# Attention projections of two tiles at a time as seven block products, with streamed weight pieces

## The chip, the cores and the metric

The kernel runs on one core of a Trainium2 chip. The metric is the device time of one execution in microseconds; several executions were timed, and one more was recorded by the hardware profiler. All data are fp32. TensorE is called PE in the profile, VectorE DVE, ScalarE ACT, GpSimd POOL and SyncE SP; SP issues most of the transfers.

## The reference

The reference runs four small networks on 64 sequences of 32 rows of 512 numbers (16 tiles of 128 rows). The kernel has them in three layers and a tail:

- layer 0: a weight chosen per sequence, a feed-forward block with two routed experts, a layer norm;
- layer 1: a gated feed-forward block with low-rank updates per sequence, and a routed low-rank block;
- layer 2: attention. Each sequence has 512 cached keys (16 pages of 32) and 32 new ones;
- the tail: a routed low-rank block, a matrix per sequence, and a last product.

The change concerns layer 2. Cut to what matters, it computes for every sequence:

```python
q, k, v = x @ Wq.T, x @ Wk.T, x @ Wv.T        # 32, 8 and 8 heads of 128 numbers
q, k = rope(rmsnorm(q) * q_norm), rope(rmsnorm(k) * k_norm)
keys, values = pages_of(cache) + [k, v]        # 544 in all, masked beyond the length
out = softmax(q @ keys.T / sqrt(128)) @ values @ Wo.T
```

Each key head serves four query heads.

## The kernel before

Layer 2 takes the heads in two halves (`HALVES`), each with 4 key heads and 16 query heads. A step is one half of the heads for one tile of 128 rows, so there are 32 steps, and two consecutive steps are a **pair** of tiles. A step has 16 **turns**, one per sequence (4) and key head (4). In each turn PE transposes the probabilities (L684, `prT_ps`), starts the scores of the turn after the next (L900, `sc`, one buffer in PSUM), and multiplies values with probabilities (L689, `po`). DVE adds the mask and finds the row's extreme (L905), ACT takes the exponential (L907), DVE the reciprocal (L909) and the scaling (L912), and ACT copies the transposed probabilities (L918). Behind every second sequence come products with the new keys' values; before them DVE copies the new values to their places (L722).

Each turn has two **slots**, in which other work is put between the instructions of the turn. Lists of slot numbers written out by hand say what goes where. That work is:

- the **projections** of the next step, by `Projection.product`. A step has six of 128x512 outputs: `v`, `k` and four groups of `q`. Each sums four products of 128x512 in a PSUM tile with tag `mm` (two buffers), two products in each of two slots. All weights of a half lie in SBUF (six tiles of 1 MB) and are loaded at the start of the half by `weights`;
- the rotation of `q` and `k` by `rotated`. ACT squares out of PSUM (L728), DVE sums the squares (L730, L731), POOL takes the inverse root (L128). DVE multiplies by the rotary tables `cos` (L741) and `sin` (L744, two halves) out of PSUM, and POOL adds and scales (L747, L748). `turned` then transposes the result on PE (`qkT_ps`), and ACT copies it (L801, L803);
- the **output product** of the pair before (`Outputs`). It already uses a scheme of seven block products in place of eight: two tiles of rows are cut into blocks of a 2x2 matrix, so is the weight, and sums of blocks are multiplied. Its weights come as pieces of 0.5 MB (`wo`), four ahead; the pieces that are sums of blocks were made in layer 1 by `sum_up` and stored in DRAM (`wo_sums`).

Keys come as 16 transfers of 64 KB per sequence on SP's queue (`load_keys`, L100), weight pieces on the same queue in a fixed order (`load_by`). Values come by four indirect transfers per sequence, which POOL issues (L715). `later` holds loads that follow in the next slots, two per slot.

PE's instructions run in the order in which they are written (`on_pe`); for the other engines the framework chooses the order from the dependencies and its own estimates.

In layer 1 `sum_up` has three parts (`rows` loads four blocks, `add` makes four sums of 128x256 on POOL (L289 to L292), `store` writes them back). Two such sums are made in each of the eight groups.

Of the kernel before, what the change touches and what calls it, by code (L numbers as in the profile page):

```python
# [33 lines left out]
P = 128  # L34
# [18 lines left out]
SCALE = 1.0 / float(np.sqrt(HD))  # L53

# [217 lines left out]
def sum_up(c, pool, sums, h, k):  # L272


    nc, a = c.nc, c.a
    H = D // 2
    w, t = [], []

    def rows():
        w.append(pool.tile([P, 4, H], F32, name="sum", bufs=3))  # L280
        for n in range(2):
            at = (h * HQP + n * HQP // 2 + k) * HD
            nc.sync.dma_start(w[0][:, 2 * n:2 * n + 2, :].rearrange("p a b -> p (a b)"),
                              a["WoT"][at:at + HD, :])

    def add():
        t.append(pool.tile([P, 4, H], F32, name="sum", bufs=3))
        (b11, b12, b21, b22), (t1, t2, t3, t4) = ([v[0][:, n, :] for n in range(4)] for v in (w, t))
        nc.gpsimd.tensor_tensor(t1, b12, b11, ALU.subtract)  # L289
        nc.gpsimd.tensor_tensor(t3, b22, b12, ALU.subtract)  # L290
        nc.gpsimd.tensor_tensor(t2, b22, t1, ALU.subtract)
        nc.gpsimd.tensor_tensor(t4, b21, t2, ALU.subtract)  # L292

    def store():
        nc.sync.dma_start(sums[h][:, k], t[0])

    return rows, add, store


def layer1(c, kp, x_in, x_out, sums):  # L300
# [12 lines left out]
    with ExitStack() as ctx:  # L313
# [193 lines left out]

        groups[0].x(0)
# [3 lines left out]
        for g, new in enumerate(groups):  # L512
            old = groups[g - 1] if g else None
            then = groups[g + 1] if g + 1 < len(groups) else None
            sum0, sum1 = (sum_up(c, sum_p, sums, *divmod(2 * g + i, HQP // 2)) for i in range(2))
            new.features(0)
            sum0[0]()
            if old:
                old.choose(0)
            new.features(1)  # L520
            if old:
                old.choose(1)
            new.features(2)
# [3 lines left out]
            sum0[1]()  # L527
            new.features(3)
# [4 lines left out]
            new.features(4)  # L533
# [6 lines left out]
            new.features(5)  # L540
            sum0[2]()
            sum1[0]()
            new.features(6)
            new.features(7)
            if then:
                then.x(0)
            new.features(8)
            if then:
                then.x(1)
            new.features(9)  # L550
            if then:
                then.firsts("x")
            sum1[1]()
            new.features(10)
            sum1[2]()
# [82 lines left out]
def attention(c, known, x_in, y_part, y_out, sums, tail):  # L638
# [13 lines left out]

    tc, nc, a = c.tc, c.nc, c.a
    half = HD // 2
    n_c = L // P
    with ExitStack() as outer:
        wvk = outer.enter_context(tc.tile_pool(name="l2_key_value_weights", bufs=1))
# [3 lines left out]
        wp = outer.enter_context(tc.tile_pool(name="l2_query_weights", bufs=1))  # L661
        op = outer.enter_context(tc.tile_pool(name="l2_output_weights", bufs=1))
# [6 lines left out]
        ws = {"v": wvk.tile([P, KC, HKP * HD], F32, name="wv"),  # L669
              "k": wvk.tile([P, KC, HKP * HD], F32, name="wk"),  # L670
              "q": [wp.tile([P, KC, D], F32, name=f"wq{g}") for g in range(HKP)]}
# [63 lines left out]
        def rotated(psrc, tab):  # L735

            src = psrc.rearrange("p (h d) -> p h d", d=HD)
            ct, st = tab
            rs = squares_and_root(src)
            r = qp.tile([P, REP, HD], F32, name="rot")  # L740
            nc.vector.tensor_tensor(r, src, ct.unsqueeze(1).to_broadcast([P, REP, HD]), ALU.mult)  # L741
# [5 lines left out]
            nc.gpsimd.tensor_tensor(r, r, tmp, ALU.add)  # L747
            last = nc.gpsimd.tensor_tensor(r, r, rs.unsqueeze(2).to_broadcast([P, REP, HD]), ALU.mult)  # L748
            return r, last.ins

        class Projection:


            def __init__(self, h, T, w):
                self.h, self.T, self.w = h, T, w
                self.r, self.acc = {}, {}
                self.first = "v"

            def load(self):
                self.xt = c.load(xp, "xt", [P, D], x_in(self.T))  # L760

            def tables(self):
                self.tabs = {}
                for n in ("q", "k"):
                    ct = qp.tile([P, 2, half], F32, name=n + "_cos")
                    st = qp.tile([P, 2, half], F32, name=n + "_sin")
                    for t, w_n, f in ((ct, norm[n][0], cos), (st, norm[n][1], sin)):
                        self.last_pool = nc.gpsimd.tensor_tensor(
                            t, w_n, f[:, self.T, :].unsqueeze(1).to_broadcast([P, 2, half]),
                            ALU.mult).ins  # L770
                    self.tabs[n] = tuple(t.rearrange("p u f -> p (u f)") for t in (ct, st))

            def x(self):
                pt = transposes("tq", "xT_ps", [self.xt[:, k * P:(k + 1) * P] for k in range(KC)])
                self.xT = xp.tile([P, KC, P], F32, name="xT")
                nc.scalar.copy(self.xT, pt)

            def product(self, what, u):

                n, g = (what, 0) if what in ("k", "v") else ("q", what)  # L780
                if what == self.first and u == 0:
                    self.qT = qp.tile([P, HKP, SEQ, REP, S], F32, name="qT")
                    self.kT = qp.tile([P, HKP, P], F32, name="kT_own")
                    self.v = qp.tile([P, HKP * HD], F32, name="v")
                if u == 0:
                    self.acc[what] = ps.tile([P, D], F32, tag="mm", bufs=2, name=f"p{n}")
                w = self.w[n][g] if n == "q" else self.w[n]
                part(self.acc[what], [(self.xT[:, k, :], w[:, k, :]) for k in (2 * u, 2 * u + 1)],
                     u == 0, u == 1)
                if u == 0:  # L790
                    return
                if what == "v":
                    nc.scalar.copy(self.v, self.acc[what])
                else:
                    self.r[what], self.last_pool = rotated(self.acc[what], self.tabs[n])

            def turned(self, what):
                r = self.r.pop(what)
                pt = transposes("tq", "qkT_ps", [r[:, m, :] for m in range(REP)])
                if what == "k":  # L800
                    nc.scalar.copy(self.kT, pt)  # L801
                else:
                    nc.scalar.copy(self.qT[:, what].rearrange("p j h s -> p h j s"),  # L803
                                   pt.rearrange("p h (j s) -> p h j s", j=SEQ))
# [11 lines left out]
        def wo_piece(h, m, u):  # L816
# [6 lines left out]
            else:  # L823
                src = sums[h][:, u * QH:(u + 1) * QH, {5: 0, 6: 1, 7: 2, 4: 3}[m], :]
# [63 lines left out]
        def scores(i, p, h, b, g):  # L888
# [7 lines left out]
            q = p.qT[:, g, b % SEQ].rearrange("p h s -> p (h s)")  # L896
# [56 lines left out]
        def weights(h, what):  # L953

            n, g = (what, 0) if what in ("k", "v") else ("q", what)
            heads = HQP if n == "q" else HKP
            at = h * heads * HD + g * D
            c.load_by(ws[n][g] if n == "q" else ws[n],
                      a[f"W{n}T"][:, at:at + D].rearrange("(k p) n -> p k n", p=P))

# [10 lines left out]
        projections = {s: Projection(h, T, ws) for s, (h, T) in enumerate(steps)}  # L971
# [47 lines left out]
        def projected(what, *then):  # L1019
            p.product(what, 0)  # L1020
            p.product(what, 1)
            for w in then:
                p.turned(w)
# [456 lines left out]
```

## Time and profile before

| what | value |
|---|---|
| median of 3 runs | 3651.27 us (3644.59 to 3653.99) |
| the profiled execution, own time | 3648.7 us |
| its span | 3646.9 us |
| granted TensorE clock | 0.998 |
| moved by DMA | 527 MB, 145 GB/s in the mean |
| layer 2, from the first to the last turn | 1087 to 3451 us |
| period of a pair of tiles | 149.4 us |

The span runs from the first to the last instruction. In a row of a group, the number behind `x` counts the instructions, then come their busy time, the mean of one in ns, and the time for which the engine stood idle before them, with what ended it. An fp32 product of PE is shown as two instructions. Consecutive instructions of an engine overlap a little, so the distance between two is less than the mean of one.

### The profile page before, as it was taken

The page shows a single profiled execution, that of the slowest core. Times are in us where ns is not written, and L with a number is a line of the kernel's source. Part 1 is how long each engine was busy: PE and PEld are TensorE (multiplying, and loading weights), DVE is VectorE, ACT ScalarE, POOL GpSimd, SP SyncE. Part 2 cuts the span into 40 slices and gives each one's busy share as a digit, 9 for nine tenths or more (in the row PEclk, how much of TensorE's full clock was granted, in tenths as well). Part 3 has the DMA queues.
Part 4 walks back from the last instruction along what each step waited for, and adds up shares of the span by engine and source line. Part 5 has one row for each costly group of instructions (what it writes and reads, how often), then busy time and mean ns, then how long its engine had stood idle before and what let it go on. Part 6 is the DMA issues. An engine that isn't in the chain of part 4 may idle for free.

```text
span 3646.9 us, 60352 instructions
## 1 busy us (share of the span) xinstructions
PE 3589.7 (98%) x19520; PEld 2665.6 (73%) x19520; DVE 1894.8 (52%) x4932; ACT 1296.2 (36%) x3046; POOL 1415.8 (39%) x1407
## 2 busy tenths in 40 slices
PE   8999999999999999999999999999999999999999
PEld 3444788888866777777777877778777788777855
DVE  5453222222236655666666656566666666666533
ACT  1111111111115544444444444444444444444311
POOL 0112430000025544555445454454555544545232
PEclk9999999999999999999999999999999999999999
DMA  5004541111124566555555565555555555556631
GB/s 211 24 27 170 171 152 55 50 45 36 38 93 133 149 186 185 155 171 153 185 183 153 181 219 179 179 151 182 174 181 169 156 186 178 170 175 201 218 97 62
DMA packets 527914, 527.15 MB, mean 145 GB/s; under 512 B 54162, under 2 KB 441234, under 8 KB 527602
## 3 DMA queue, kind: packets, MB, share of 16 engines
q1 hardware_dynamic: 480882, 371.21, 32.9%
q0 software_dynamic: 44416, 147.88, 12.6%
q10 hardware_dynamic: 2304, 4.20, 0.3%
q8 instruction: 159, 2.61, 0.3%
q14 instruction: 153, 1.25, 0.1%
HBM read 493.72 MB, written 29.36 MB: 143 GB/s over the span
## 4 chain that ended last, share of the span: by engine, by line
PE 85%; DVE 8%; ACT 2%; DMA 2%; issue 1%; SPq 1%; DVEq 0%; POOL 0%; another core or an unknown queue 0%; ACTq 0%; POOLq 0%
PE po L689 12%; PE sc L900 11%; PE gate_up L342 10%; PE pq L689 9%; PE py L689 9%; PE prT_ps L684 5%; PE pz L342 5%; PE po L1249 3%; PE ph L124 3%; PE pk L689 3%; PE pv L689 3%; PE pd L249 2%; DVE own_vt L722 2%; PE po L342 2%; DVE pr L905 1%; PE qkT_ps L684 1%
## 5 line engine op out<-in xcount | busy, mean ns | idle before, releaser
L715 POOL DMA_INDIRECT vt<-in_v_rows,v_rows x512 | 499.9, 976 | 594.6 <-PE po L689 484.2
L907 ACT ACTIVATE pr<-pr,low 128x544 f32<-128x544 f32 x512 | 383.5, 749 | 703.5 <-DVE low L905 630.4
L689 PEld LDWEIGHTS po<-prT,vt 128*128 128x128 f32 x4096 | 531.3, 192 | 111.1 <-issue 80.7
L900 PE MATMUL sc<-kt,qT 128*128 128x288 f32 (+1 forms) x2048 | 556.3, 394 | 5.5 <-ACT qT L803 1.7
L689 PE MATMUL po<-prT,vt 128*128 128x128 f32 x4096 | 543.9, 276 | 9.5 <-ACT prT L918 6.3
L905 DVE CUSTOM_DVE_ANT_0 pr<-sc,mask 128x544 f32<-128x544 f32 x512 | 368.8, 720 | 321.8 <-PE sc L900 288.5
L900 PEld LDWEIGHTS sc<-kt,qT 128*128 128x128 f32 x2048 | 370.6, 190 | 156.0 <-issue 62.0
L689 PE MATMUL pq<-wq,xT 128*128 128x512 f32 x1024 | 480.6, 592 | 0.0
L918 ACT COPY prT<-prT_ps 128x512 f32<-128x512 f32 x512 | 295.3, 577 | 202.1 <-PE prT_ps L684 147.6
L912 DVE TENSOR_SCALAR pr<-pr,low 128x512 f32<-128x512 f32 x512 | 341.1, 666 | 15.1
L684 PE MATMUL prT_ps<-ident,pr 128*128 128x128 f32 x2048 | 311.2, 275 | 0.1
L689 PEld LDWEIGHTS pq<-wq,xT 128*128 128x128 f32 x1024 | 185.8, 190 | 132.4 <-issue 125.3
L909 DVE RECIPROCAL low<-low 128x1 f32<-128x1 f32 x512 | 83.5, 163 | 340.8 <-ACT pr L907 305.7
L684 PEld LDWEIGHTS prT_ps<-ident,pr 128*128 128x128 f32 x2048 | 238.1, 142 | 7.9 <-issue 0.3
L689 PE MATMUL py<-wo,oT 128*128 128x256 f32 x1024 | 241.4, 379 | 0.0
L128 POOL TENSOR_TENSOR rs<-rs,minus_half 128x4 f32<-128x4 f32 x160 | 169.2, 1058 | 162.9 <-DVE rs L731 158.1
L910 ACT ACTIVATE own_pr<-pr,low 128x32 f32<-128x32 f32 x512 | 164.0, 320 | 131.0 <-DVE low L909 120.3
L747 POOL TENSOR_TENSOR rot<-rot,swapped 128x512 f32<-128x512 f32 x160 | 205.0, 1281 | 5.1 <-DVE swapped L744 3.9
L689 PEld LDWEIGHTS py<-wo,oT 128*128 128x128 f32 x1024 | 187.6, 190 | 21.9
L722 DVE COPY own_vt<-v 32x128 f32<-32x128 f32 x512 | 173.1, 338 | 38.3 <-PE po L689 13.9
L689 PE MATMUL py<-wo,o_sum 128*128 128x256 f32 x768 | 181.3, 379 | 2.1 <-DMA wo<-wo_sums 1.3
L426 DVE TENSOR_TENSOR sg<-sg,gate_up 128x256 f32<-128x256 f32 (+1 forms) x88 | 37.0, 421 | 276.0 <-ACT sg L425 276.0
(226 smaller groups left out, 5192.9 us busy)
## 6 DMA issues: line engine op xcount, KB each, us to landing
kt<-in_kT SPq DMA_DIRECT2D x2048, 64.0 KB
wo<-wo_sums SPq DMA_DIRECT2D x128, 512.0 KB
wo<-in_WoT SPq DMA_DIRECT2D x96, 512.0 KB
xt<-x SPq DMA_DIRECT2D x48, 256.0 KB
A<-in_A SPq DMA_DIRECT2D x64, 152.0 KB
sets<-in_cond0T SPq DMA_DIRECT2D x32, 256.0 KB
sum<-in_WoT SPq DMA_DIRECT2D x32, 256.0 KB
wo_sums<-sum SPq DMA_DIRECT2D x16, 512.0 KB
```

What stands on the lines that cost most here:

```text
L128: self.nc.gpsimd.tensor_tensor(t, t, self.minus_half[:, :n], ALU.pow)
L342: c.on_pe(nc.tensor.matmul(out, lhsT, rhs, start=start, stop=stop))
L684: c.on_pe(nc.tensor.transpose(pt[:, m, :], piece, c.ident))
L689: c.on_pe(nc.tensor.matmul(out, lhsT, rhs, start=first and i == 0, stop=last and i == len(pairs) - 1))
L715: nc.gpsimd.indirect_dma_start(out=vts[b % 2][:, n, :], out_offset=None, in_=a["v_rows"], in_offset=bass.IndirectOffsetOnAxis(ap=rows[h][: ...
L722: nc.vector.tensor_copy(own_vts[b % 2][g * S:(g + 1) * S, g % 2, :], v[j * S:(j + 1) * S, g * HD:(g + 1) * HD])
L747: nc.gpsimd.tensor_tensor(r, r, tmp, ALU.add)
L900: c.on_pe(nc.tensor.matmul(sc[:, lo + n * PSIZE:lo + m * PSIZE].rearrange("p (n k) -> p n k", k=PSIZE), q, kt[:, n:m, g, :], start=True, s ...
L905: nc.vector.tensor_tensor_reduce(pr[:, :NK], sc[:, lo:lo + NK], masks[h, b], -SCALE, 3.0e38, ALU.add, ALU.min, low[:, 0:1])
L907: nc.scalar.activation(pr[:, :NK], pr[:, :NK], AF.Exp, bias=low[:, 0:1], scale=-1.0, accum_out=low[:, 1:2])
L912: nc.vector.tensor_scalar(pr[:, :L], pr[:, :L], low[:, 2:3], None, ALU.mult)
L918: nc.scalar.copy(prT, pt)
```

## The change

A pair of tiles is projected together. The 2x2 blocks are the two tiles (rows) by the two halves of the 512 input numbers; the weight's blocks are the two halves of the input by two column blocks of 512. The column blocks form three groups (`GB = 3`) per half of the heads: `k` with `v`, and `q` in two groups of two. Each group takes seven products of 256 by 512 (two 128x512 products each) instead of eight.

- `x_sums` makes the four sums of the tiles' blocks on POOL (128x256 each). `product` multiplies one of them with a weight piece. Its result is copied by ACT (products 1 and 5) or added to an earlier one by DVE out of PSUM (2, 6, 3, 7 and 4); after products 3 and 7 POOL adds two results in SBUF. Results lie in SBUF, and `rotated` now works there in place.
- Weights no longer stay in SBUF. They come as 21 pieces of 0.5 MB per pair, four ahead, by `wp_piece`: blocks of the weights, or sums of blocks made in layer 1.
- In layer 1, `all_sums` makes 40 sums instead of 16, five per group.
- All projections of pair n+1 stand in the first step and the second step of pair n, at slots 16 to 51 of 64 (8 to 52 in the first pair). The output products of pair n-1 stand at slots 0 to 15 and 53 to 61, in the last pair at 1 to 43. Before the first turn, all of the first pair is projected.
- The tail's weights take the places of other tiles, and are loaded earlier in the last pair.

```diff
-        def rotated(psrc, tab):
-            src = psrc.rearrange("p (h d) -> p h d", d=HD)
+        def rotated(t, tab):
+            src = t.rearrange("p (h d) -> p h d", d=HD)
             ct, st = tab
             rs = squares_and_root(src)
-            r = qp.tile([P, REP, HD], F32, name="rot")
-            nc.vector.tensor_tensor(r, src, ct.unsqueeze(1).to_broadcast([P, REP, HD]), ALU.mult)
             tmp = wk.tile([P, REP, HD], F32, name="swapped")
...
-            nc.gpsimd.tensor_tensor(r, r, tmp, ALU.add)
-            last = nc.gpsimd.tensor_tensor(r, r, rs.unsqueeze(2).to_broadcast([P, REP, HD]), ALU.mult)
+            nc.vector.tensor_tensor(src, src, ct.unsqueeze(1).to_broadcast([P, REP, HD]), ALU.mult)
+            nc.gpsimd.tensor_tensor(src, src, tmp, ALU.add)
+            nc.gpsimd.tensor_tensor(src, src, rs.unsqueeze(2).to_broadcast([P, REP, HD]), ALU.mult)
...
+        def wp_tile(name="wp", **kw):
+            return op.tile([P, K2, D], F32, name=name, tag="wp", bufs=4, **kw)
+
+        def wp_piece(h, g, m):
+            w = wp_tile()
+            if m in (1, 2, 3):
+                k, n = {1: (0, 0), 2: (1, 0), 3: (1, 1)}[m]
+                src = column_blocks(a, h, g)[n][k * K2 * P:(k + 1) * K2 * P, :] \
+                    .rearrange("(k p) n -> p k n", p=P)
+            else:
+                src = sums["in", h][:, g, {5: 0, 6: 1, 7: 2, 4: 3}[m]]
+            c.load_by(w, src)
+            return w
...
+            def x_sums(self):
...
+                nc.gpsimd.tensor_tensor(s1, x21, x22, ALU.add)
+                nc.gpsimd.tensor_tensor(s2, s1, x11, ALU.subtract)
+                nc.gpsimd.tensor_tensor(s3, x11, x21, ALU.subtract)
+                nc.gpsimd.tensor_tensor(s4, x12, s2, ALU.subtract)
...
+            def product(self, g, m):
+                (x11, x12), (_, x22) = self.blocks
+                lhs = {1: x11, 2: x12, 3: self.s[3], 4: x22, 5: self.s[0], 6: self.s[1], 7: self.s[2]}[m]
+                w = wps.pop(0)
+                acc = ps.tile([P, D], F32, tag="mm", bufs=2, name="pq" if g else "pkv")
+                part(acc, [(lhs[:, k, :], w[:, k, :]) for k in range(K2)], True, True)
+                d = self.d = {} if m == 1 else self.d
+                if m in (1, 5):
...
+                    nc.scalar.copy(d[at], acc)
                     return
...
+                nc.vector.tensor_tensor(d[to], acc, d[other], ALU.add)
+                if m == 3:
+                    nc.gpsimd.tensor_tensor(d[0, 1], d[0, 1], d[1, 1], ALU.add)
+                elif m == 7:
+                    to = (1, 1)
+                    nc.gpsimd.tensor_tensor(d[1, 1], d[1, 1], d[1, 0], ALU.add)
+                if m != 6 and not (g == 0 and to[1]):
+                    rotated(d[to], self.tabs["q" if g else "k", to[0]])
...
         p = projections[0]
         p.load()
         p.tables()
-        for what in ("v", "k") + GROUPS:
-            weights(0, what)
-        for b in range(2):
-            new_keys(0, b)
-            load_keys(0, b)
-        p.x()
+        for _ in range(4):
+            next_wp()
+        new_keys(0, 0)
+        load_keys(0, 0)
+        p.x(0)
+        p.x(1)
+        p.x_sums()
...
+                        ats = ((16, 17, 20, 22, 24, 26, 28), (32, 33, 35, 36, 38, 40, 41),
+                               (43, 44, 46, 47, 48, 49, 51))
+                        then = ((0, 0, 0, 27), (0, 1, 0, 37), (1, 0, 0, 42), (1, 0, 1, 45), (1, 1, 1, 50),
+                                (1, 1, 0, 52), (2, 0, 0, 53), (2, 0, 1, 57), (2, 1, 1, 59), (2, 1, 0, 60))
...
+                    for g in range(GB):
+                        for m, i in zip(p.ORDER, ats[g]):
+                            at(i, partial(p.product, g, m), partial(later.append, next_wp))
```

`ORDER` is (1, 2, 5, 6, 3, 7, 4). `ats` holds the slot of each product, `then` that of each transposition.

## The prediction

> **What bounds the kernel now.** I read the page's busy times first, then its groups, then the busy time by stretch over the attention layer (1060 to 3450 us), then the chain of waits and the timelines of VectorE and GpSimd in one period.
>
> ```profile
> PE 3589.7 (98%) x19520; PEld 2665.6 (73%) x19520; DVE 1894.8 (52%) x4932; ACT 1296.2 (36%) x3046; POOL 1415.8 (39%) x1407
> L689 PE MATMUL pq<-wq,xT 128*128 128x512 f32 x1024 | 480.6, 592 | 0.0
> L905 DVE CUSTOM_DVE_ANT_0 pr<-sc,mask 128x544 f32<-128x544 f32 x512 | 368.8, 720 | 321.8 <-PE sc L900 288.5
> L912 DVE TENSOR_SCALAR pr<-pr,low 128x512 f32<-128x512 f32 x512 | 341.1, 666 | 15.1
> L747 POOL TENSOR_TENSOR rot<-rot,swapped 128x512 f32<-128x512 f32 x160 | 205.0, 1281 | 5.1 <-DVE swapped L744 3.9
> L748 POOL TENSOR_TENSOR rot<-rot,rs 128x512 f32<-128x512 f32 x160 | 172.2, 1077 | 6.3
> ```
>
> TensorE is busy 98% of the span and hardly ever idle; the other engines have time. Each fp32 product is two records, so pq's 1024 are 512 products.
>
> ```profile
> 2457.40:2606.80 149.40, 149.34 (x842) 116.34 (x841) 94.32 (x241) 69.94 (x167) 78.13 (x77) 1.00 0.56 174
> 2150.00:2160.00 10.00, 10.00 (x50) 6.79 (x49) 8.67 (x20) 5.06 (x13) 5.52 (x6) 1.00 0.79 259
> 2160.00:2170.00 10.00, 10.00 (x61) 7.41 (x61) 8.46 (x24) 4.65 (x10) 8.71 (x10) 1.00 0.94 321
> 2180.00:2190.00 10.00, 8.65 (x48) 7.42 (x48) 4.56 (x12) 3.57 (x11) 3.88 (x4) 1.00 0.84 261
> 3405.00:3420.00 15.00, 14.25 (x90) 12.68 (x88) 6.34 (x19) 6.54 (x17) 5.25 (x6) 1.00 0.79 238
> ```
>
> The columns are the stretch, its length, busy PE, PE loads, DVE, ACT, POOL, then clock, DMA share and GB/s. The first line is one pair of tiles: 149.4 us, TensorE full, VectorE at 63%. Rows two and three show VectorE at 86% over 20 us with TensorE still full. The fourth holds the layer's longest wait for a weight piece (1.35 us). The last has no projections, and TensorE loses 5% of it.
>
> ```profile
> 2160.21 1.72 PE pq L689 x4
> 2161.92 1.98 PE po L689 x24
> 2163.91 0.59 PE prT_ps L684 x4
> 2166.21 0.92 PE sc L900 x4
> 2167.57 1.73 PE py L689 x8
> ```
>
> The chain gives true pitches (means overlap): two 128x512 products take 1.72 us, so one is 0.86. A turn is scores 0.92, transposes 0.44 and values 0.89, and with its share of the own part 2.41 us.
>
> ```profile
> 2458.59 1.03 DVE L912 TENSOR_SCALAR pr<-pr,low 128x512 f32<-128x512 f32 x1
> 2475.18 0.49 DVE L912 TENSOR_SCALAR pr<-pr,low 128x512 f32<-128x512 f32 x1
> 2458.30 1.04 POOL L748 TENSOR_TENSOR rot<-rot,rs 128x512 f32<-128x512 f32 x1
> ```
>
> The same VectorE instruction takes 1.03 us when it starts beside a GpSimd tensor operation, ending 0.28 us after it, and 0.49 alone.
>
> **What the Trainium skill says.** "SBUF — State Buffer", section "Who interferes with whom": VectorE and GpSimd share one port pair as an exclusive lock, and a VectorE instruction with two SBUF inputs contends with a GpSimd instruction that reads SBUF. The L912 lines agree for the scaling form. For two SBUF inputs no run here shows it: o_sum (L846) ran only beside an indirect DMA, 0.73 against 0.69 us. "PSUM — Partial Sum Buffer", section "Engine vs sequencer instructions": VectorE's and GpSimd's queues are strict FIFO; the wait tables fit (the reduction L730 waits 120.5 us in all for squares, with the queue behind it). "DMA: Bandwidth & Descriptors", section "Issuing engines are not separate DMA queues": all transfers end on the same 16 engines; so the value gathers of GpSimd compete with the new pieces.
>
> **The change, part by part.**
>
> *Products removed.* A pair of tiles has 2 x 6 x 4 = 48 products of 128x512, 41.3 us at 0.86. Afterwards 3 groups x 7 x 2 = 42, 36.1 us. That is 5.16 us in each of 16 pairs: **82.6 us**, all on the engine that sets the end. Transposes stay as many.
>
> *VectorE.* Five additions of 128x512 out of PSUM per group are new, 15 per pair. L491 has this form, 0.69 us, about 0.62 in sequence: 9.3 us per pair. The ten rotations keep their instructions but read SBUF twice (swapped, cos). Their three calls each now contend: GpSimd's tensor work will hold half of the crowded stretch, a blocked call waits about 0.6 us (half a 1.28 or 1.07), so 30 x 0.5 x 0.6 = 9 us; bounds 0 (no contention, as the L846 lines would allow) and 30 x 0.6 = 18.
>
> *Where it lands.* The products stand in slots 16 to 51 of 64, that is 18 turns. TensorE there: 18 x 2.41 + 36.1 + 5 transposes of 0.44 = 81.7 us. VectorE: per turn 2.18 (a 32nd of the 94.3 us, less 20 for rotations and 4.5 for the outputs), 39.2; additions 9.3; ten rotations of 2.0 in sequence, 20; contention 9: 77.5 us, 95%. With the contention at its bounds it is 84% to 106%. 86% cost nothing above, so this stretch is the critical point. Some lag runs off in slots 52 to 63 and 0 to 15, where VectorE has about 38 us of work for 60. The scores' one PSUM buffer allows VectorE a lag of about a turn less its own work, some 3.5 us, before TensorE stops at L900. I take 1.8 us lost per pair in the 15 pairs that project for the next: **27 us back**; 0 to 10 per pair as bounds.
>
> *Waits added.* In groups 1 and 2, products 3 and 7 put a GpSimd addition (1.28) between the VectorE addition and the square on ScalarE (0.59): four chains per pair. Behind the reduction on VectorE wait L905 and L912 of the next turns, for which TensorE waits. The price is in the 1.8. On the other side, an accumulator in PSUM is now freed after one 0.69 us read, not after a rotation.
>
> *GpSimd.* Six additions of 1.28 and four of 128x256 at 0.73 are 10.6 us per pair on 78: 89 of 144 us, 62%. A turned tile is due at least six slots (13 us) after its product, a rotation needs 3.4: hidden, unless the value gathers (0.98 each, 32 per pair) fall between. The rotary tables stay as many.
>
> *ScalarE.* Four more copies at 0.58: 72 of 144 us, hidden.
>
> *DMA.* 21 pieces of 0.5 MB are 11.0 MB per pair, on 26.0 (174 GB/s x 149.4): 37 MB in 144 us, **257 GB/s**. Between 2140 and 2210 us seven windows of the present kernel average 269 GB/s and TensorE lost 1.35 us. Pieces are asked for four products, some 14 us, ahead; I take no more than is in the 1.8, bounds 0 and 3 us per pair. SP issues 16 key pieces in 8.55 us: 68 us per pair, with 35 weight pieces at 0.39 some 82 of 144, so its queue doesn't bound. The 6 us chain piece at 2181 us, where the second half's weights arrive, goes: **-1.4 us**.
>
> *Layer 1.* Forty sums instead of 16. Each is four additions of 0.73: 24 x 2.9 = 70 us more on a GpSimd that has 83 of 660 us to do there, and 25 MB more for DMA. The 16 sums now run ahead, between 404 and 507 us, and TensorE is full in their first 83 us (83.00) at 232 GB/s; forty would go on so to about 650. The gathers of the next group stand behind them on GpSimd's queue, x loads and stores behind the sums' stores on SP's (47 us of wait in 14 stores). A group is 82 us long: hidden; I take 2 us, bounds 0 and 20.
>
> *Start of the attention.* Now 27.7 us pass from the first transpose to the first turn. Afterwards the start holds two tiles: 36.1 us of products, which is no loss in itself. But only four pieces are ready; the fifth stands behind one sequence's key pieces (8.5 us of issue), while four products last 6.9 us. Then 8.9 MB of pieces and about 3 MB of keys and values come within 36 us, 330 GB/s, near the 345 that the first 30 us of the program reach. GpSimd has some 40 us of rotations, tables and sums. I take **8 us**, bounds 0 and 20.
>
> *Last pair.* No projection is left there to fill gaps: 112 us of work at the 2.5% that the last 60 us lose now: **3 us**, bounds 0 and 8.
>
> *Sum.* 82.6 - 27 + 1.4 - 2 - 8 - 3 = 44 us. The profiled execution has 3646.9 of span and 3648.7 in all, so 3604.7; it lies 2.6 below the median of the runs, 3651.3. For the median: **3607**.
>
> **The rivals.**
>
> *VectorE becomes the bound.* If contention holds at 9 us and VectorE's queue waits cannot be filled beyond the 86% seen, slots 16 to 51 need 77.5 / 0.86 = 90.1 us instead of 81.7: 8.4 lost per pair, 126 us in 15. Then 126 + 13 - 84 = 55 us slower: **3706**. It decides from 4.7 us per pair on (84 - 13 = 71 us of gain, over 15). For it: the chain of waits already runs along VectorE from 2220 to 2247 us. Against it: TensorE stayed full there, and the underloaded slots beside it take up lag.
>
> *All hidden.* VectorE's lag drains, the start costs 4 and the last pair nothing: 82.6 + 1.4 - 4 = 80 us: **3571**. For it speak 149.34 of 149.40 and the early release of PSUM.
>
> *The streamed pieces come late.* Queue order rather than rate: a 0.5 MB piece behind 1 MB of keys and another piece, 3 us lost per pair, beside the 1.8 that VectorE costs: 45 us, so the gain is gone: **3652**. The seven windows speak against.
>
> That the change doesn't do what it says is not one: seven products of two blocks each are written out.
>
> **How the numbers follow.** A run cannot tell apart less than about 0.3% (11 us). My forecast has 0.58, its own range 3580 to 3640; all hidden 0.10; late pieces 0.08; VectorE as the bound 0.24. Faster is 0.66 (the first two, less a tail); same 0.09 (late pieces and that tail); slower 0.25. The range 3572 to 3698 leaves out less than 2 in 10, mostly above.
>
> **What would show it.** A pair's period near 146 us; 1344 records of projection where 1536 were; VectorE near 110 us per pair; DMA near 255 GB/s. A swapped mean above 0.414 shows the port contention, waits of sc for L905 the VectorE bound, waits for wp the late pieces. A period of 149 or more would make the forecast wrong, and a projection pitch other than 0.86 its base.

## The result, and the profile after

The changed kernel takes 3910.59 us (median of 4 runs, 3907.81 to 3912.11), the kernel before 3647.93 beside it: a ratio of 1.0717, with a 95% interval of 1.0699 to 1.0736. It is slower by 263 us, where 44 us of gain were forecast. The lines of the page that answer to those of before:

```profile
PE 3619.6 (93%) x19328; PEld 2693.9 (69%) x19328; DVE 2026.1 (52%) x5172; ACT 1336.6 (34%) x3110; POOL 1687.6 (43%) x1663
...
L987 DVE TENSOR_SCALAR pr<-pr,low 128x512 f32<-128x512 f32 x512 | 310.2, 606 | 11.5
L772 POOL TENSOR_TENSOR projected<-projected,swapped 128x512 f32<-128x512 f32 x160 | 203.1, 1269 | 171.8 <-DVE rs L757 170.5
...
L768 DVE TENSOR_TENSOR swapped<-projected,q_sin 128x256 f32<-128x256 f32 x256 | 126.7, 517 | 174.7 <-POOL projected L865 139.4
```

The 192 records of products are gone (19520 to 19328), yet TensorE is busy 30 us longer, in a span that is 259 us longer: 229 us more of idle time, and 112 us of work more than the products left (30 plus 82.6). Most of the 112 is clock: experiment 15, with the same products at a mean clock of 0.996 in place of 0.962, has 3535.5 us of TensorE work, 84 less. VectorE has the same share as before, 52%, so no engine became the bound by its work. L987 is even shorter than before (606 ns against 666). But the last row waits 139 us for a GpSimd addition (L865), and L772 waits 172 where L747, the same operation before, waited 5.

Landmarks in the two timelines say where the 259 us lie (a turn begins with its transposes `prT_ps`, a pair with its first turn): up to the first transpose of the attention 42.0 (1059.80 to 1101.84), from there to the first turn 46.3, the first pair 10.6, the 14 pairs behind it 169.8, the last pair -8.0, the rest -1.6. One of these pairs by stretch (columns as before), and what TensorE waited for in it (total, times, longest):

```profile
2619.30:2779.70 160.40, 149.35 (x831) 117.18 (x830) 101.41 (x254) 72.42 (x170) 90.01 (x86) 0.96 0.72 227
```

```profile
PE sc L975 <- DVE low L980: 5.4, 2, 4.2
PE po L715 <- ACT prT L993: 5.0, 1, 5.0
PE qkT_ps L710 <- ACT qT L878: 0.7, 1, 0.7
```

11.1 us idle, where the pair before had 0.06. The work itself takes 149.35 us, where 143.9 were due (149.04, the mean of the 14 pairs before, less 5.16): most of the other 5.4 us is clock (0.96; at 1.00 a pair with the same work takes 144.66 in experiment 6). One of the two stalls, in the timelines of GpSimd, VectorE, ScalarE and TensorE of an earlier pair:

```profile
2550.55 1.27 POOL L862 TENSOR_TENSOR projected<-projected 128x512 f32<-128x512 f32 x1 [5.80 <-DVE projected L860]
2551.98 1.22 POOL L741 DMA_INDIRECT vt<-in_v_rows,v_rows  x1 [0.16 <-PE prT_ps L710]
2553.50 0.95 POOL L741 DMA_INDIRECT vt<-in_v_rows,v_rows  x1 [0.30 <-issue]
2554.75 0.95 POOL L741 DMA_INDIRECT vt<-in_v_rows,v_rows  x1 [0.30 <-issue]
2555.73 1.05 POOL L130 TENSOR_TENSOR rs<-rs,minus_half 128x4 f32<-128x4 f32 x1
2556.97 1.02 POOL L741 DMA_INDIRECT vt<-in_v_rows,v_rows  x1 [0.19 <-issue]
2558.01 1.27 POOL L772 TENSOR_TENSOR projected<-projected,swapped 128x512 f32<-128x512 f32 x1
2559.24 1.27 POOL L865 TENSOR_TENSOR projected<-projected 128x512 f32<-128x512 f32 x1
2560.46 1.04 POOL L773 TENSOR_TENSOR projected<-projected,rs 128x512 f32<-128x512 f32 x1
```

```profile
2560.54 1.25 DVE L768 TENSOR_TENSOR swapped<-projected,q_sin 128x256 f32<-128x256 f32 x1 [4.61 <-POOL projected L865]
```

```profile
2560.54 0.63 ACT L754 ACTIVATE squares<-projected 128x512 f32<-128x512 f32 x1 [6.50 <-POOL projected L865]
2561.07 0.73 ACT L982 ACTIVATE pr<-pr,low 128x544 f32<-128x544 f32 x1
```

```profile
2558.79 1.88 PE L715 MATMUL pq<-wp,xT 128*128 128x512 f32 x4
2565.64 2.08 PE L715 MATMUL po<-prT,vt 128*128 128x128 f32 x8 [4.97 <-ACT prT L993]
```

The addition L865 stands on GpSimd's queue behind four gathers, a root and the rotation before. At the heads of their queues VectorE's `swapped` and ScalarE's square wait for it; behind the square stands the exponential of a score that is long ready (L982, 0.73 us of work), behind that TensorE's `po`. When `po` comes, its eight records take 2.08 us; with no stall ahead of them they take 1.05. The Trainium skill, "TensorE: Matmul & The Clock Gate", section "Part 1: The HAM clock gate", says that an idle window of about 3.4 us halves the array's clock until it has been busy as long again. This trace agrees on the pace: 4.97 us of wait, then work at half pace. From the start of this `po` to the end of the products behind it 5.72 us pass where 3.04 are usual; 2.7 us lost would be some 5.4 at half pace, an estimate, and so longer than the page has it. In experiment 14 a wait of 3.02 us was already enough: four records of `sc` take 1.92 us behind it where 1.08 is usual.

### The profile page after: what moved, and what is told of

Same layout as the page of the kernel before. It is cut to its first block, busy times and chain, and to the rows that moved or that the text cites. A ratio compares the mean times of both kernels' runs of the same rounds, so it can differ in the third digit from the quotient of the medians.

```text
span 3906.1 us, 61517 instructions
## 1 busy us (share of the span) xinstructions
PE 3619.6 (93%) x19328; PEld 2693.9 (69%) x19328; DVE 2026.1 (52%) x5172; ACT 1336.6 (34%) x3110; POOL 1687.6 (43%) x1663
## 4 chain that ended last, share of the span: by engine, by line
PE 72%; DVE 7%; issue 6%; POOL 5%; DMA 3%; SPq 3%; ACT 2%; DVEq 0%; another core or an unknown queue 0%; POOLq 0%; ACTq 0%
PE po L715 12%; PE py L715 10%; PE sc L975 10%; PE pq L715 7%; PE gate_up L367 6%; PE prT_ps L710 5%; PE pkv L715 4%; PE po L1323 3%; PE ph L126 3%; PE pz L367 3%; PE pd L251 2%; SPq L102 2%; PE qkT_ps L710 2%; DVE projected L860 1%; DVE swapped L768 1%
## 5 line engine op out<-in xcount | busy, mean ns | idle before, releaser
L741 POOL DMA_INDIRECT vt<-in_v_rows,v_rows x512 | 519.1, 1014 | 608.4 <-PE po L715 477.2
L975 PE MATMUL sc<-kt,qT 128*128 128x288 f32 (+1 forms) x2048 | 572.9, 403 | 90.9 <-DVE low L980 82.9
L715 PE MATMUL po<-prT,vt 128*128 128x128 f32 x4096 | 564.0, 282 | 86.6 <-ACT prT L993 84.4
L982 ACT ACTIVATE pr<-pr,low 128x544 f32<-128x544 f32 x512 | 382.9, 748 | 512.7 <-DVE low L980 411.1
L987 DVE TENSOR_SCALAR pr<-pr,low 128x512 f32<-128x512 f32 x512 | 310.2, 606 | 11.5
L772 POOL TENSOR_TENSOR projected<-projected,swapped 128x512 f32<-128x512 f32 x160 | 203.1, 1269 | 171.8 <-DVE rs L757 170.5
L715 PE MATMUL pq<-wp,x_sums 128*128 128x512 f32 x512 | 240.4, 593 | 0.7 <-DVE projected L860 0.7
L754 ACT ACTIVATE squares<-projected 128x512 f32<-128x512 f32 x160 | 101.1, 632 | 354.9 <-POOL projected L865 175.0
L768 DVE TENSOR_TENSOR swapped<-projected,q_sin 128x256 f32<-128x256 f32 x256 | 126.7, 517 | 174.7 <-POOL projected L865 139.4
L715 PE MATMUL py<-wo,o_sum 128*128 128x256 f32 x768 | 201.8, 411 | 8.2 <-issue 8.2
L715 PE MATMUL pq<-wp,xT 128*128 128x512 f32 x384 | 197.4, 640 | 1.8 <-DVE projected L860 0.9
```

What stands on the lines that cost most here:

```text
L715: c.on_pe(nc.tensor.matmul(out, lhsT, rhs, start=first and i == 0, stop=last and i == len(pairs) - 1))
L741: nc.gpsimd.indirect_dma_start(out=vts[b % 2][:, n, :], out_offset=None, in_=a["v_rows"], in_offset=bass.IndirectOffsetOnAxis(ap=rows[h][: ...
L768: nc.vector.tensor_tensor(tmp[:, :, lo:lo + half], src[:, :, hi:hi + half], st[:, lo:lo + half].unsqueeze(1).to_broadcast([P, REP, half]), ...
L772: nc.gpsimd.tensor_tensor(src, src, tmp, ALU.add)
L975: c.on_pe(nc.tensor.matmul(sc[:, lo + n * PSIZE:lo + m * PSIZE].rearrange("p (n k) -> p n k", k=PSIZE), q, kt[:, n:m, g, :], start=True, s ...
L982: nc.scalar.activation(pr[:, :NK], pr[:, :NK], AF.Exp, bias=low[:, 0:1], scale=-1.0, accum_out=low[:, 1:2])
```

## The experiments

The kernel of before beside these runs took 3632 to 3648 us; compare ratios. "Period" is a pair's time by landmarks (149.4 before, 160.5 after), "first turn" that of the attention (1087 and 1176).

**1. The two GpSimd additions of seven products on VectorE.**

```
-  nc.gpsimd.tensor_tensor(d[0, 1], ...)   # product 3; likewise product 7
+  nc.vector.tensor_tensor(d[0, 1], ...)
```

> The two additions after products 3 and 7 run on VectorE instead of GpSimd; all else as in the changed kernel (3911 us, pair period 160.5 us). Theory A (a rotation that follows a GpSimd addition stands at the head of VectorE's and ScalarE's queues until GpSimd gets to that addition, and the scores' softmax waits behind it): the stalls of 4 to 5 us before scores and values go, the clock stays at 1.00, the pair period falls to 145 to 149 us and the time to 3680 to 3740 us. Theory B (VectorE has too much work, port contention included): VectorE gets 3.7 us per pair more to do, so the period stays at 160 or grows to 165: 3910 to 3980 us. Theory C (late pieces or SP's queue): no change, 3905 to 3915 us.

3764.37 us, ratio 1.0344 (1.0326 to 1.0361); periods 151.5 to 153. More work for VectorE, and 9 us less for each pair: the place in the queues is the cost, not the work. Over the 14 pairs 47 us are lost to the kernel before, in place of 170. The total stops short of theory A's 3740. One reason is in the trace: VectorE now waits for `L772` of the rotation before, since `swapped` is one buffer (30 us in nine pairs).

**2. No streamed pieces.** After the first four none is loaded; the products read old pieces.

```
+            if len(held) < 4:
+                held.append(wps_to_come.pop(0)())
+            elif wps_to_come:
+                wps_to_come.pop(0)
...
+            held.append(held.pop(0))
+            wps.append(held[-1])
```

> Left out: the weight pieces after the first four are not loaded; every product multiplies with one of the first four pieces in turn. Instructions of the engines are as in the changed kernel, 164 MB of transfers fewer. Theory A: the pair period stays at 158 to 161 us, the start of the attention gets some 5 to 15 us shorter, 3885 to 3910 us. Theory C (the stream slows the pairs): the period falls to 150 us or less, 3750 us or less.

3889.97 us, ratio 1.0684 (1.0663 to 1.0706); periods 160.1 to 162.6, in the mean 1.0 us less than in the changed kernel (161.8, in which one pair has 172.2). The stream isn't the cause.

**3. The forty sums alone, in the kernel of before.** `all_sums` and layer 1's loop of the changed kernel; the 24 new sums have no reader.

> The kernel before with layer 1's part of the change alone: 40 sums of blocks are made and stored there, of which the attention reads only the 16 of the output weights. Theory A1 (SP's queue stands at the stores of the sums, which wait for GpSimd, and the next group's x loads are behind them): TensorE waits some 32 us for x in layer 1, the attention starts at 1095 to 1105 us instead of 1060, 3685 to 3695 us in all. Rival (the sums are hidden, and what delays layer 1 in the changed kernel is its other order of transfers): 3645 to 3655 us.

3683.31 us, ratio 1.0117 (1.0097 to 1.0137): 42 us, TensorE waits 33.3 us in layer 1 for its x, and the pairs stay at 149.

**4. The sums' stores by GpSimd.** `nc.sync.dma_start(dst, t[0])` becomes `nc.gpsimd.dma_start`.

> The stores of the sums are issued by GpSimd's queue instead of SP's; all else as in the changed kernel. Theory A1 (SP's queue blocked at the stores): the waits of TensorE for x in layer 1 (32 us) go, the attention starts at 1060 to 1070 us instead of 1102, about 3870 us. Rival (40 sums are too much for GpSimd or for the transfers beside layer 1): the start stays within 10 us of 1102, 3900 to 3925 us.

3911.41 us, ratio 1.0743 (1.0722 to 1.0765): no gain. SP now waits at the row loads for the stores (54.8 and 33.7 us), and TensorE for x 41.7 us in place of 32.2. The reading that fits: three buffers chain load, addition and store, and whichever of them stands on SP holds what is behind it.

**5. Layer 1's x loads by ScalarE** (with the edit of 1, to be read against it).

```
+  (nc.scalar if self.g else nc.sync).dma_start(x, x_in(...))
```

> As the first experiment (additions on VectorE), and the x loads of layer 1 issued by ScalarE's queue, so that they no longer stand behind the sums on SP's queue. The first experiment took 3764 us, its TensorE waited 29 us for x, its attention started at some 1100 us. Theory A1 in the form that the experiment with the stores on GpSimd leaves (SP's queue stands behind the sums' chain of load, addition, store and reuse of three buffers, wherever the store is issued, and x behind it): the waits for x go, the attention starts at 1060 to 1070 us, 3720 to 3735 us in all. Rival (the transfers themselves are too slow beside 42 MB of sums, or another load is late next): the start stays above 1085 us, 3750 us or more.

3767.72 us, ratio 1.0339 (1.0321 to 1.0356): nothing gained over 1. TensorE's wait for x is gone, but one for `hwT`, a ScalarE copy, is there instead (31.0 us, longest 18.2): the x load goes out at 519.53 us, right behind a sum's first operation on GpSimd (518.66, 0.72 us), and the copy stands behind it on ScalarE's queue. The trace puts ScalarE's idle time there down to the rows of the sums (29.3 us, up to 519.90); so the sums' chain seems to hold x on either queue. By what dependency is not shown.

**6. Four rotations later.** The additions stay on GpSimd; the rotation of what they make is written three places behind product 3 and four behind product 7.

```
+                    if m in (3, 7):
+                        self.late.append(rotation)
...
+                            if g and m in (3, 7):
+                                at(i + (3 if m == 3 else 4), p.late_rotation)
```

> As the changed kernel, with the additions on GpSimd, but the four rotations that follow such an addition are put 3 or 4 slots later, so that VectorE and ScalarE come to them when GpSimd is done. No work is taken away or moved to another engine. Theory A (the place in the queues, not the work): the long stalls go, the pair period falls from 160.5 to 147 to 153 us, 3710 to 3800 us in all. Theory B (too much work on VectorE or GpSimd): the period stays at 157 us or more, 3860 us or more.

3780.67 us, ratio 1.0371 (1.0351 to 1.0392); a pair by stretch:

```profile
2539.50:2691.00 151.50, 144.66 (x830) 113.35 (x828) 102.83 (x253) 71.80 (x169) 89.48 (x85) 1.00 0.76 240
```

The same work on every engine, other places: 9 us less in each pair, clock 1.00, TensorE's work at 144.7. The 14 pairs lose 46 us to the kernel before, in place of 170. With 1 this shows the cause of most of the 169.8 us.

**7. Program order on SP in layer 1** (with 6). Loads and stores of sums and of x go through `load_by`, each tied behind the one before.

```
-  nc.sync.dma_start(w[0][:, n, :], block)
+  c.load_by(w[0][:, n, :], block)      # likewise dst, xt, x_out
```

> The kernel of e6_late_rotations, with one thing more: in layer 1 every row load and store of a sum, every x load and every x store is tied behind the transfer that the program gives before it (load_by), so that SP issues them in the program's order: five sums to a group over all eight groups, where the traces so far show all forty sums issued within the first three groups, between 413 and 660 us, and ahead of the x stores and x loads of those groups. Theory L (the loss of layer 1 is the order on SP: the sums have no tie to TensorE, are put in front, and the x stores and loads wait behind their chain of three buffers): xT_ps waits for xt fall from 30 us to under 4, the start of attention comes back from about 1100 to 1060 to 1068, total 3738 to 3752. Rival (the forty sums' own work, 88 us of GpSimd additions and 40 MB of loads beside the layer, costs the time wherever they stand): the start of attention stays over 1085 and the total over 3765.

3729.55 us, ratio 1.0262 (1.0244 to 1.0279): 1.1% under 6, and the attention's first transpose is at 1065.6 instead of 1099.9 (before: 1059.8), as theory L had it. That the total is under its range comes from the last pair, which is 10 us shorter too (120.6 to 110.4); why is not shown. What SP did in the changed kernel:

```profile
522.48 3.29 SPq L294 DMA_DIRECT2D out_sums<-sum  x2
525.86 0.38 SPq L517 DMA_DIRECT2D x<-o  x1
526.34 0.73 SPq L87 DMA_DIRECT2D xt<-x  x1
```

and TensorE's timeline beside it, with what ended the wait:

```profile
529.84 1.11 PE L402 MATMUL xT_ps<-ident,xt 128*128 128x128 f32 x4 [13.90 <-DMA xt<-x]
```

The x load is the third in this row; TensorE stood 13.9 us. TensorE's waits for x in layer 1, and SP's waits (400 to 680 us), are

```profile
PE xT_ps L402 <- DMA xt<-x: 32.2, 4, 13.9
```

```profile
SPq L294 <- POOL sum L291: 101.6, 37, 6.2
```

The framework chooses SP's order and had nothing that ties a sum to TensorE. So it put the sums of all eight groups into three, each store waiting for its additions, ahead of the x transfers. In program order SP itself still waits (110.7 us for `o`, 58.2 for sums) and hardly anything waits for SP: of TensorE's 32.2 us for x in layer 1, 2.3 are left.

**8. Both cures of the pairs** (7 with 1).

> e7_sums_in_program_order with the two GpSimd additions of each seven products on VectorE besides, as in e1_adds_on_dve: both cures of the pairs at once. Theory A (what is left in the pairs, 152 us against some 144.7 of TensorE work, is again VectorE's queue held by GpSimd's): periods of 146 to 149, total 3665 to 3705. Rival (with the rotations late, the rest is the rotations' own chain over GpSimd, rs by GpSimd's power and the last two operations, which the turn waits for, wherever the additions are made): periods of 150.5 to 152.5, total 3725 to 3755.

3692.52 us, ratio 1.0161 (1.0144 to 1.0178); periods 149.2: the total is theory A's, the period just above its upper edge of 149. The 14 pairs lose 10 us to the kernel before. In a pair 4.6 us of waits are left:

```profile
PE sc L985 <- DVE low L990: 2.1, 2, 1.2
PE own_prT_ps L712 <- ACT qT L888: 1.6, 1, 1.6
PE qkT_ps L712 <- ACT qT L888: 0.9, 1, 0.9
```

**9. The first keys behind the eighth piece** (8, and `load_keys(0, 0)` moved behind `products(0, ms[:4])`).

> e8_order_late_on_dve, with the sixteen kt loads of the first head moved from ahead of the fifth piece of the projections' weights to behind the eighth, at the start of attention alone. Theory S (the 5.6 us wait of the sixth product and the 5 us of slow products after it come from the sixteen issues on SP in front of the piece): wait for wp in this stretch under 1.5 us, total 6 to 12 us under e8_order_late_on_dve. Rival (the pieces are late by their own transfers, 0.5 MB each, four at a time, or the kt loads are now late for the first scores): within 3 us of e8_order_late_on_dve, with sc waiting for kt at the start.

3697.64 us, ratio 1.0172 (1.0155 to 1.0189): no gain. The wait moves from `pkv` (7.1 us) to `pq` (6.9 for `WqT`), as the first rival had it.

**10 to 12. Places of turns, then the start.** In 10, `then` becomes (26, 36, 42, 48, 54, 58, 62, 66, 68, 70), each with its transposition; 11 adds that the pieces' pool lies where layer 1 frees memory early (and the keys as in 9); 12 adds four ScalarE operations in place of the last operation of the first pair's rotations.

> The kernel of e8_order_late_on_dve with the turns of the rotated projections in other places of the handwritten order, for all pairs but the first to be projected: six of the ten to even places of the step (behind which scores and a weighted sum come before the next transposes), the four of the second tile up to ten places later, since its scores come half a pair later. Nothing is added or removed. Theory T (the 4.7 us that TensorE still loses in a pair of e8 are turns right ahead of other transposes, which wait for ScalarE's copy of qT in the same PSUM buffers: 1.6 at own_prT, 0.9 at qkT, and scores held by VectorE 1.2 and 0.9): periods of 146 to 147.5, total 3655 to 3675. Rival (each of these waits moves to the next instruction that needs the same copy): periods over 148.5, total over 3680.

> e10_turn_places with the start of attention changed: the pool of the streamed pieces lies where layer 1's earliest freed buffers are, so that SP issues the first four pieces ahead of layer 1's last two x stores, and the first kt loads stand behind the eighth piece. Theory S2 (10 us of waits for pieces and some 5 us of slow products behind them): the first four products do not wait, waits for wp in the start of attention under 3 us in place of 10, total 8 to 14 us under e10_turn_places. Rival (the pieces from the fifth on come no faster than 0.5 MB in about 2.5 us, and the wait moves to them): under 5 us gained.

> e11_first_pieces_early with the last operation of the rotation (the multiplication with rs) on ScalarE, in four operations of 128x128, for the first pair's projections alone, where three turns wait 11 us for GpSimd's. Theory G (at the start GpSimd's chain of 36 us, ten rotations of 1.06 + 1.28 + 1.27, is what the turns wait for): these waits under 4 us, total 5 to 9 us under e11_first_pieces_early. Rival (VectorE, with 2.2 us of work to each product of 1.72, is next): under 3 us gained.

3823.33, 3818.56 and 3816.43 us; ratios 1.0523 (1.0506 to 1.0541), 1.0513 (1.0496 to 1.0531), 1.0506 (1.0488 to 1.0523). In 10, moving nine of the ten numbers costs 131 us: places 54, 62 and 70 stand right behind `own_prT`'s transposes, so `qkT` waits for that copy (59.1 us in all), `sc` waits 64.2 us where it waited 34.6, and `py` waits in five pairs. From the attention's first transpose to the first turn 11 gains 2.5 us and 12 another 2.3: in 11 the pieces' wait moves on again (9.5 us at `pq`), in 12 GpSimd's goes. So all three came out as their rivals said, 10 far beyond it. The gains of 11 and 12 in the total, 5 and 2 us, are less than the 11 us that runs can tell apart.

**13. Only four turns moved** (12 with 37 to 36, 45 to 48, 53 to 49, 50 to 51 from the first order; keys in four parts).

> e12_first_scales_by_act with the turns back in the places of e8_order_late_on_dve except four: 37 to 36, 45 to 48, 53 to 49 and 50 to 51, so that none stands right ahead of own_prT's transposes (places 6, 14, 22 and so on) and none right behind them; and the first sixteen kt loads in four parts between the products of the start. Theory T2 (the loss left in the pairs is the turn right ahead of own_prT): own_prT waits of 23 us fall under 5, periods of 146.5 to 147.5; first turn at 1115 to 1125 against 1134.5; total 3640 to 3660. Rival (the wait moves to another instruction, as in e10): periods of 149 or more, total 3675 to 3690, the start's gain alone.

3839.49 us, ratio 1.0525 (1.0507 to 1.0542). The `own_prT` waits are gone, but periods are 160.5 and the total is above both expectations, for a reason that neither had: TensorE's `py`, SP and ScalarE in their timelines.

```profile
2410.06 3.75 PE L718 MATMUL py<-wo,o_sum 128*128 128x256 f32 x8 [7.82 <-issue]
```

```profile
2394.22 8.29 SPq L102 DMA_DIRECT2D kt<-in_kT  x16
2402.61 1.17 SPq L102 DMA_DIRECT2D wo<-out_sums  x2
2403.89 0.91 SPq L973 DMA_DIRECT2D y_part<-y  x2
```

```profile
2409.59 0.37 ACT L959 COPY y<-py 128x256 f32<-128x256 f32 x1 [5.15 <-DMA y_part<-y]
```

The trace names no releaser for `py`. Read from the rows: the y tiles are one pair's, their store stands behind sixteen key loads, ScalarE's copy waits for the store, and the next `py` for the PSUM buffer that the copy reads.

**14. The y stores by GpSimd, four places earlier** (with 13).

```
-  nc.sync.dma_start((y_out if self.h else y_part)(T), y)     # place 70
+  nc.gpsimd.dma_start((y_out if self.h else y_part)(T), y)   # place 66
```

> e13_few_turns_moved with one thing changed: the two stores of y of each pair go out by GpSimd's queue at place 2 of the next pair, in place of SP's at place 6, where they stand behind sixteen kt loads. Theory Y (py with o_sum waits for a PSUM buffer, whose ScalarE copy waits for the y tile, whose store waits on SP): the py waits of 112 us, 13 times, fall under 12 us, periods from 160.5 to 147.5 to 150, total 3655 to 3690. Rival (py waits for the wo piece or for GpSimd's o_sum): the periods stay over 158.

3684.28 us, ratio 1.0141 (1.0124 to 1.0158); periods 150.2, and no wait of `py` is left. So it was the store; whether its queue or its place was at fault is not shown, since both were changed. One such wait (8.15 us at 1499.7, a period of 172.2) is in the changed kernel too.

**15. No two rotations within two places** (with 14).

```
+  at(i + {3: 2, 7: 3, 4: 5}[m], p.late_rotation)
```

> e14_y_stores_by_gpsimd with the three rotations after the products 3, 7 and 4 of each query group put 2, 3 and 5 places behind their products, in place of 3, 4 and 0, so that no two stand within two places of each other (3.6 us of GpSimd each, one swapped buffer). Theory R (the wait of 3 us of sc once a pair is VectorE behind a rotation that waits for GpSimd's last): this wait under 1 us, periods 1.5 to 3 us under e14's. Rival (it is the products' additions and the rotations' own work on VectorE that delay the extreme): periods within 0.7 us of e14's.

3669.56 us, ratio 1.0100 (1.0083 to 1.0117), the best of the line, and still 1.0% slower than the kernel before. The wait of `sc` falls from 64.0 to 26.0 us in all, but that of `po` rises from 4.3 to 22.6 and `pq` now waits 19.2. So the periods fall only from 150.2 to 149.4, nearer the rival. In the mean of the 14 pairs TensorE's idle time stays as it was (4.35 and 4.33 us) and its work falls from 145.91 to 145.16: what was gained is clock (0.99 to 1.00); where one wait of 3.0 us stood, there are several of at most 1.9. The first pair gains 5 us more (145.8 to 140.8). A pair:

```profile
2462.40:2611.80 149.40, 145.07 (x830) 113.65 (x829) 104.59 (x260) 72.04 (x170) 83.50 (x82) 1.00 0.75 242
```

and its waits:

```profile
PE sc L990 <- DVE low L995: 1.5, 2, 1.2
PE pq L718 <- DVE projected L868: 1.5, 2, 1.3
PE po L718 <- ACT prT L1008: 1.2, 1, 1.2
```

Against the kernel before, in the mean of these pairs, TensorE's work fell by 3.9 us (149.04 to 145.16), and its idle time rose by 3.7. That the products can't be fitted in without such waits is not shown; no order that was tried did it, and what an order without them would look like stays open.

## Why the prediction was wrong

**The saving was right.** 19328 records, and pairs with 144.4 to 145.2 us of TensorE work (8 and 15) where 144 were forecast. VectorE has 101 to 105 us per pair, for 110 expected; DMA 227 to 248 GB/s, for 257, and the pieces cost the pairs 1 us each at most (2).

**"Waits added" is the step that failed.** It named the chain, four GpSimd additions between product and square, with L905 and L912 behind, and then gave it no price of its own: "The price is in the 1.8." A pair lost 16.5 us (160.4 for 143.9), 11.0 idle and the rest mostly clock, outside the bounds of 0 to 10. Either cure of this one wait takes about 9 of them away (1 and 6), both together 11 (8). The working added up busy times over 18 turns and compared sums. But a queue that stands still 4.6 us at its head is not a matter of 95%: VectorE is busy 63% of the pair in both kernels. The wait should have been priced along GpSimd's queue: four gathers at about 1 us, a root at 1.05 and a rotation at 1.27 ahead of an addition of 1.27 are 7.6 us of work, against some 3.5 of lag that the text itself allowed for. "Unless the value gathers (0.98 each, 32 per pair) fall between" was the case, noted under GpSimd and weighed as hidden.

**The clock was left out.** The stall shown above, of 4.97 us, cost 2.7 us more in slow work, and the prediction has no term for that.

**Contention: the mechanism holds, the share was too large.** 9 us per pair were charged, half of 30 calls at 0.6. `swapped` rose from 414 to 517 ns in the mean, 1.6 us over a pair's 16. The Trainium skill, "SBUF — State Buffer", section "Who interferes with whom", says that two SBUF inputs contend with a GpSimd instruction that reads SBUF, and the trace agrees: of the 480 calls of the two rotary multiplications (`swapped` and `cos`), the 34 that began while GpSimd's multiplication with `rs` (L773) was running took mostly 1.25 us, for 0.42 (`swapped`) and 0.68 (`cos`) otherwise, and ended 0.3 to 0.55 us after it; the 1.25 us of `swapped` beside L773 in the timelines above is one. The 31 that began up to 0.13 us ahead of it took their usual time, and L773 longer. A blocked call costs 0.8 us, more than the 0.6 charged, but only 7% are blocked, not half, so the term is 1.6 us. So the rival "VectorE becomes the bound" came out on the right side (its 126 us against some 240 in 15 pairs) for the wrong reason: 1 gives VectorE more work and is faster. That queues are strict FIFO (the Trainium skill, "PSUM — Partial Sum Buffer", section "Engine vs sequencer instructions"), was the sentence to calculate with: in the timelines above `swapped` holds VectorE's queue for 4.61 us, the square ScalarE's for 6.50.

**Layer 1: 2 us with a bound of 20, measured 42.** The step named the danger, x loads and stores behind the sums' stores on SP, and dismissed it because a group is 82 us long. It was right that the forty sums would run ahead, to about 650 us (measured: 404 to 660). What failed is "hidden": the length of a group doesn't help an x load that stands behind stores which wait for GpSimd (101.6 us in all). TensorE waited 32.2 us for x, four times, and without that order 34 of the 42 us are gone (3 and 7).

**Start: 8 us, measured 46.3 to the first turn.** By the waits in the two timelines some 17 are products and transposes that were only moved (42 products of 0.86 for 24, and about 2), 19 more waiting, 10 slower clock. The pieces (5.6 us) were foreseen; the turns' waits for `qT` (5.3 and 3.2) had no price. The longer is the same chain as in the pairs: in front of ScalarE's copy of `qT` stands a square that waits 4.85 us for L865.

**Last pair: 3 us, measured about 13.** It has 24 products less than before, 20.6 us, and is only 8.0 us shorter. TensorE is idle for 10.5 us, 10.2 of it in `po` waiting for ScalarE's `prT`, nine times; in 15 the pair is 19 us shorter than before. What holds ScalarE there was not tested.

**In sum:** forecast -44, measured +259 in the profiled runs. Of the 303 us between, 40 are layer 1's, some 23 the start's (46.3 less the 8 of the forecast and 15.5 of products only moved there), 10 the last pair's, and some 230 the 15 other pairs'. Of these, 1 and 6 show that 124 come from the place of the GpSimd additions, and 36 more go when both cures are made (8). Most of the rest is the forecast gain of the pairs, which no run reached: with each order the short waits took back what the products gave.

## What to carry to other kernels

Price a new wait along the queue of the engine that ends it, with the longest row of other work that can stand there, and compare it with the lag that the bounding engine's buffers allow; shares of busy time say nothing on it. An engine with 40% idle time is not free when it stands between two in-order queues that the bound depends on: move the short operation to the waiting engine, or write its reader later. Background work that nothing ties to the critical engine may be ordered ahead of all that is; tie it to the program's order.

## What was not expected of the hardware

A stall costs twice on this TensorE: after 4.97 us of waiting eight records of `po` took 2.08 us where 1.05 is usual, and four records of 128x512 3.16 where 1.88 is usual. After 3.02 us (14) four records of `sc` took 1.92 for 1.08; the waits of at most 1.9 us in 15 left the clock of a pair at 1.00. Over the changed kernel this came to some 84 us (3619.6 us of TensorE work against 3535.5 in 15), beside 229 of added idle time.

For a VectorE operation with two SBUF inputs beside GpSimd's L773 it mattered which began first. Behind a running L773 `swapped` took up to 1.26 us; when it began just ahead, it took 0.40 to 0.43, and L773 1.17 to 1.28 where its median is 1.04.
